# Splitting the attention's row maxima into bf16 parts on GpSimd instead of VectorE

## The chip, the cores and the metric

The kernel runs on one core of a Trainium2 chip. The metric is the device time of one execution in microseconds (us). A core has five engines that each run their own queue of instructions in order and wait for each other by semaphores: TensorE (PE in the profile, its weight loads PEld), VectorE (DVE), ScalarE (ACT), GpSimd (POOL) and SyncE (SP, which here only issues DMAs).

## What is computed

Six residual steps on x of shape 16 x 512 x 128, float32. The change concerns the second, causal attention with 16 heads of width 8 that share 4 key and value heads. Cut to what matters:

```python
x = x + 0.5 * ffn0(layernorm(x))     # per-feature networks of width 16 (called kan)
x = x + attn(layernorm(x))           # below
x = x + 0.5 * ffn0(layernorm(x))
x = x + 0.5 * experts(layernorm(x))  # each of 8 experts takes its 128 best tokens
x = x + recurrence(layernorm(x))
x = x + 0.5 * experts(layernorm(x))

# attn
att = einsum('bhqd,bhkd->bhqk', q, k) * HD ** -0.5   # q and k rotated, HD = 8
att = where(causal, att, lowest)
y = einsum('bhqk,bhkd->bhqd', softmax(att), v) @ Wo
```

The softmax needs each query's largest score subtracted before the exponential.

## The kernel before

**Packed operands.** To keep float32 accuracy with bf16 matmuls, q and k are each split into three bf16 parts, and the nine products are laid along the contraction: 9 x 8 = 72 rows. A packed tile of queries QP (10 of them, one per batch row and key head) and of keys KP (3 of them) has 72 rows of parts, and further down, at rows 96 to 98 (`MXR = 96`, L31), three rows for the row maximum. In QP these three rows hold the three bf16 parts of *minus* the maximum of each query; in KP they hold ones (`keys_cleared`, L503). So the matmul of scores over rows 0 to 98 (`ROWS`, L188) gives score minus maximum at once, and the exponential needs no bias per query.

**Two passes.** For each of the 16 batch rows b, `maxima` (L597) multiplies the 72 rows into PSUM (tile ps_sc, L611), and VectorE reduces each bank to row maxima (L616 with the causal mask, L621 for several heads at once). After each half (two of four key heads, 8 heads) `max_rows` (L625) makes the three parts: ms part 0 is the bf16 of minus the maximum, r the rest, part 1 the bf16 of r, part 2 what then remains. TensorE transposes ms into ps_m (L642), VectorE copies that to mr (L644), and SP sends it through DRAM into rows 96 to 98 of two QP tiles (L649, L651). One batch row later, `weights` (L657) multiplies 99 rows (ps_st, L669), ScalarE takes the exponential into pt (L672), and GpSimd zeroes the upper triangle of the diagonal block (L674). `outputs` (L680) multiplies pt by the values (ps_av, L692).

**The order of work.** The order on TensorE, ScalarE, VectorE and GpSimd is written out by the kernel. A loop of turns, 44 per batch row (one for each of 11 banks of each key head), issues one bank of `weights` of row b and one bank of `maxima` of row b + 1. Then `turn` (L1104) gives one step first to each generator in the list urgent (`max_rows` and `outputs`) and then to each in sides: the stages of other rows, such as `kan` (L329), `attn_in` (L415, rotation and splitting of q and k, with GpSimd sums rope_a, L440, rope_ka, L463, and `parts`, L393), `stage_out`, the layer norms (`norm`, L280) and the top-8 routing. A step asks by `need(...)` (L221) for a share of an engine's budget per turn, and waits for a later turn if what is left is too little:

```python
MOST = {"pe": 1.5, "dve": 1.15, "act": 0.85, "pool": 1.45}   # L218
while paced[0] and any(w > room[e] for e, w in work.items()):
    yield
```

The rope sums ask for pool=1.25, the steps of `parts` for 1.15 to 1.3, a layer norm for dve=0.6 and pool=1.4. A PSUM bank of the two that the side stages share is asked for by `bank` (L243). Half 0 of row b + 1 is finished in the middle of the turns of row b, half 1 at the start of those of row b + 1.

After the 16 rows come the experts and the recurrence, with no attention work left (from about 960 us on).

The functions that are touched, and what calls them:

## Time and profile before

| | |
|---|---|
| median of 3 runs | 1685.1 us (1683.93 to 1688.63) |
| profiled execution | 1679.07 us, span 1677.3 us |
| mean granted TensorE clock | 0.979 of full speed |
| instructions in the profile | 35404 |
| attention's matmuls of scores, ps_sc L611 and ps_st L669 | 259.6 and 258.5 us busy, 1024 each |
| row maxima, L616 on VectorE | 315.0 us busy, 512 |
| masking, L674 on GpSimd | 252.7 us busy, 704 |

The profile lists busy times by engine, groups of equal instructions by line of the kernel (out<-in by tile names, count, busy us, mean ns, and the idle time before them with what ended it), and the chain of work that ended last. A timeline row has start and duration in us, the engine, the line and the tiles; in brackets the idle time before it and what it waited for. "Busy" for TensorE comes from modelled ends: a matmul's row is longer than the distance at which the next can start, so distances between starts are read for its waits.

### The profile page before, as it was taken

Reading aid. Unit: us, or ns where it says so; the run is one execution under the profiler, and the core shown is the slowest. Engines: PE = TensorE matmul, PEld = TensorE weight load, DVE = VectorE, ACT = ScalarE, POOL = GpSimd, SP = SyncE. Lnnn points to the kernel's source line nnn. Section 1 sums busy time; section 2 is a strip of 40 time slices with the busy share of each in tenths; the row PEclk is TensorE's granted clock in tenths of the full one; section 3 lists DMA queues with packets and bytes.
Section 4 is the critical chain, followed back from the end, with each engine's and each line's share of the span. In section 5 each row is a group of like instructions: output and inputs, shape, how many; then the busy total and the mean of one; then the engine's idle time right before and its main releaser. Section 6 shows DMA issues by size and latency. Waiting matters only on the chain.

```text
span 1677.3 us, 35404 instructions
## 1 busy us (share of the span) xinstructions
PE 1573.0 (94%) x12943; PEld 1093.7 (65%) x12943; DVE 1124.6 (67%) x3606; ACT 1002.3 (60%) x2000; POOL 1023.6 (61%) x1486
## 2 busy tenths in 40 slices
PE   5689999999999999999999799999999999999998
PEld 2234444444444544455444399888998889999998
DVE  6578878888888888888986146843469544672222
ACT  3446677787777877777777565444443434444454
POOL 2635557556665556565634757657766668667774
PEclk9779999999999999999999799999999999999999
DMA  4210111111101110111122114223323233333333
GB/s 123 67 63 26 56 50 40 33 42 57 53 30 40 49 57 23 40 52 56 35 81 62 30 40 78 58 52 76 64 59 64 58 61 73 67 64 75 70 77 58
DMA packets 103093, 94.87 MB, mean 57 GB/s; under 512 B 13197, under 2 KB 91478, under 8 KB 102678
## 3 DMA queue, kind: packets, MB, share of 16 engines
q1 hardware_dynamic: 76060, 67.65, 13.1%
q0 software_dynamic: 26048, 24.93, 9.4%
q8 instruction: 102, 1.67, 0.4%
q14 instruction: 73, 0.60, 0.1%
q10 hardware_dynamic: 810, 0.02, 0.0%
HBM read 59.00 MB, written 37.49 MB: 58 GB/s over the span
## 4 chain that ended last, share of the span: by engine, by line
PE 71%; DVE 19%; ACT 5%; issue 3%; POOL 2%; DMA 1%; DVEq 0%; SPq 0%; POOLq 0%; ACTq 0%
PE ps_h L935 12%; PE ps_y L950 11%; PE ps_av L692 7%; PE ps_st L669 6%; PE ps_sc L611 5%; DVE below L616 5%; PE acc L968 4%; PE ps_kg L365 4%; PE ps_s L338 3%; PE ps_t L318 3%; DVE ln_st L287 2%; ACT pt L672 2%; PE ps_ko L386 2%; PE ps_h L1076 2%; PE ps_h L1075 1%
## 5 line engine op out<-in xcount | busy, mean ns | idle before, releaser
L674 POOL TENSOR_SCALAR_AFFINE_SELECT pt<-pt 128x128 f32<-128x128 f32 (+2 forms) x704 | 252.7, 366 | 331.4 <-ACT pt L672 326.6
L672 ACT ACTIVATE pt<-ps_st 128x512 f32<-128x512 f32 (+1 forms) x704 | 378.8, 563 | 99.8 <-PE ps_st L669 94.0
L616 DVE CUSTOM_DVE_ANT_0 below<-ps_sc,causal 128x512 bf16<-128x512 f32 (+1 forms) x512 | 315.0, 615 | 80.1 <-PE ps_sc L611 64.8
L937 ACT ACTIVATE mo<-ps_h 128x512 f32<-128x512 f32 x256 | 152.8, 597 | 290.4 <-PE ps_h L935 288.5
L859 POOL DMA_INDIRECT xg<-xnd,tokI x256 | 252.3, 986 | 80.9 <-issue 45.0
L669 PE MATMUL ps_st<-qp,kp 99*128 99x512 bf16 (+3 forms) x1024 | 258.5, 305 | 21.7 <-ACT pt L672 20.8
L935 PE MATMUL ps_h<-xin,mw 128*128 128x128 f32 x2048 | 278.3, 279 | 0.0
L950 PE MATMUL ps_y<-mw,mo 128*128 128x128 f32 x2048 | 271.1, 275 | 0.4 <-DVE mo L959 0.4
L611 PE MATMUL ps_sc<-kp,qp 72*128 72x512 bf16 (+3 forms) x1024 | 259.6, 305 | 11.6 <-DVE maxs L616 6.6
L935 PEld LDWEIGHTS ps_h<-xin,mw 128*128 128x128 f32 x2048 | 249.7, 192 | 6.1 <-issue 3.2
L950 PEld LDWEIGHTS ps_y<-mw,mo 128*128 128x128 f32 x2048 | 249.1, 192 | 1.5 <-DVE mo L959 1.3
L982 POOL DMA_INDIRECT sum<-ye,tokI x124 | 201.4, 1624 | 63.4 <-ACT ye L953 22.7
L669 PEld LDWEIGHTS <-kp 99*128 99x128 bf16 x1024 | 95.1, 100 | 181.7 <-issue 164.4
L371 ACT ACTIVATE kan_h<-kan_s,rbias,kw 128x512 f32<-128x512 f32 x256 | 205.7, 812 | 3.8 <-PE ps_kg L365 3.8
L692 PE MATMUL ps_av<-pt,va 128*32 128x512 f32 (+3 forms) x2048 | 165.5, 441 | 0.0
L621 DVE TENSOR_REDUCE maxs<-ps_sc 128x2 f32<-128x512 f32 (+1 forms) x192 | 130.1, 685 | 34.9 <-PE ps_sc L611 34.4
L611 PEld LDWEIGHTS <-qp 72*128 72x128 bf16 x1024 | 96.2, 99 | 79.8 <-issue 57.2
L956 DVE TENSOR_TENSOR mo<-mo 128x128 bf16<-128x128 f32 x132 | 38.2, 290 | 129.4 <-ACT mo L941 129.1
L692 PEld LDWEIGHTS ps_av<-pt,va 128*32 128x32 f32 x2048 | 53.7, 109 | 94.9 <-issue 44.1
L968 PE MATMUL acc<-mo 128*128 128x128 bf16 x1584 | 111.3, 219 | 3.1 <-DVE mo L956 3.0
L968 PEld LDWEIGHTS <-mo 128*128 128x128 bf16 x1584 | 98.6, 98 | 19.9 <-issue 18.6
L294 POOL TENSOR_TENSOR ln_rstd<-ln_rstd,mhalf 128x4 f32<-128x4 f32 x96 | 101.1, 1053 | 8.0
(197 smaller groups left out, 2362.2 us busy)
## 6 DMA issues: line engine op xcount, KB each, us to landing
qp<-qs SPq DMA_DIRECT2D x64, 288.0 KB
xnd<-kan_x SPq DMA_DIRECT2D x32, 256.0 KB
sum<-x SPq DMA_DIRECT2D x31, 256.0 KB
qs<-qpart SPq DMA_DIRECT2D x48, 128.0 KB
kp<-ks SPq DMA_DIRECT2D x48, 96.0 KB
x<-in_L_attn_x_dram SPq DMA_DIRECT2D x16, 256.0 KB
mw<-in_L_ffn_w_dram SPq DMA_DIRECT2D x16, 256.0 KB
xg<-xnd,tokI POOLq DMA_INDIRECT x256
```

The costliest lines, as they stand in the source:

```text
L371: nc.scalar.activation(h, sk[half], AF.Relu, bias=rbias[:, half, v : v + 1], scale=kw1[:, half, v : v + 1])
L611: nc.tensor.matmul(v[:, u, 0:n], lhsT=qp[r][0 : 9 * HD, g, bass.ts(c, P)], rhs=kp[0 : 9 * HD, r, 0:n], start=alone, stop=(u == len(gs) - 1 ...
L616: nc.vector.tensor_tensor_reduce(below[:, 0:n], v[:, 0, 0:n], causal[:, S - n : S], 1.0, LOWEST, ALU.add, ALU.max, accum_out=maxs[:, c, h ...
L669: nc.tensor.matmul(v[:, u, 0:n], lhsT=kp[ROWS, r, bass.ts(c, P)], rhs=qp[r][ROWS, g, c * P : S], start=True, stop=True)
L672: nc.scalar.activation(o, v[:, :, 0:n], AF.Exp, scale=HD ** -0.5)
L674: nc.gpsimd.affine_select(out=dg, in_=dg, compare_op=ALU.is_ge, fill=0.0, base=0, pattern=[[0, len(gs)], [1, P]], channel_multiplier=-1)
L692: nc.tensor.matmul(po[32 * g : 32 * g + 32, c * P : S], lhsT=va[:, c, r, :], rhs=pt[:, g, OFF[c] : OFF[c] + n], start=(c == 0), stop=(c == ...
L859: nc.gpsimd.indirect_dma_start(out=xgs[i // E % 2][:, i % E, :], out_offset=None, in_=xnd[b], in_offset=bass.IndirectOffsetOnAxis(ap=tokI[ ...
L935: nc.tensor.matmul(pst[:, f, :], lhsT=mw1[e][:, bass.ts(f, P)], rhs=xins[i // E % 2][:, i % E, :], start=True, stop=True)
L950: nc.tensor.matmul(py, lhsT=hs[u][:, f, :], rhs=mw2[e][:, f, :], start=(f == 0), stop=(f == NF - 1))
L968: nc.tensor.matmul(acc[:, c, :], lhsT=sels[u][:, bass.ts(c, P)], rhs=yes[u][:, w, :], start=(e == 0 and c == 0 and w == 0), stop=(e == las ...
L982: nc.gpsimd.indirect_dma_start(out=sums[k, b], out_offset=bass.IndirectOffsetOnAxis(ap=tokI[g][:, n : n + 1], axis=0), in_=ye[:, b % 2 * ( ...
```

## The change

GpSimd makes the parts instead of VectorE, the parts keep the sign of the maximum, and the keys' three rows hold minus ones instead of ones. The two requests to the turn's budget ask for GpSimd instead of VectorE. Since `max_rows` steps before the side stages in a turn, the order of the side stages' work follows from what is left of each budget.

```diff
@@ -503,7 +503,7 @@
         def keys_cleared(i):
 
             cleared(KP[i])
-            nc.vector.memset(KP[i][MXR : MXR + 3, :, :], 1.0)
+            nc.vector.memset(KP[i][MXR : MXR + 3, :, :], -1.0)
@@ -625,16 +625,15 @@
         def max_rows(b, half, maxs):
 
             H2 = NH // 2
-            yield from need(dve=0.45)
+            yield from need(pool=0.5)
             ms = w2p.tile([P, NT, 3, H2], BF16, name="ms")
             r = w2p.tile([P, NT, H2], F32, name="ms_r")
-            nc.vector.tensor_scalar_mul(ms[:, :, 0, :], maxs, -1.0)
-            nc.vector.scalar_tensor_tensor(r, in0=maxs, scalar=-1.0, in1=ms[:, :, 0, :],
-                                           op0=ALU.mult, op1=ALU.subtract)
-            yield
-            yield from need(dve=0.45)
-            nc.vector.tensor_copy(ms[:, :, 1, :], r)
-            nc.vector.tensor_sub(ms[:, :, 2, :], r, ms[:, :, 1, :])
+            nc.gpsimd.tensor_copy(ms[:, :, 0, :], maxs)
+            nc.gpsimd.tensor_tensor(r, maxs, ms[:, :, 0, :], ALU.subtract)
+            yield
+            yield from need(pool=0.5)
+            nc.gpsimd.tensor_copy(ms[:, :, 1, :], r)
+            nc.gpsimd.tensor_tensor(ms[:, :, 2, :], r, ms[:, :, 1, :], ALU.subtract)
             yield
             yield
             pm = yield from bank([3 * H2, NT, P], BF16, "ps_m", 0.3)
```

The changed file is one line shorter from there on, so L640 and later of the kernel before are one less in it.

## The prediction

> **What bounds the kernel now.** I read the page's busy table and its chain first, then the table of engine times for one steady batch, then the groups by shape, and last the timeline around two sets of row maxima.

> The page:

> ```profile
> PE 1573.0 (94%) x12943; PEld 1093.7 (65%) x12943; DVE 1124.6 (67%) x3606; ACT 1002.3 (60%) x2000; POOL 1023.6 (61%) x1486
> ...
> PE 71%; DVE 19%; ACT 5%; issue 3%; POOL 2%; DMA 1%; DVEq 0%; SPq 0%; POOLq 0%; ACTq 0%
> ```

> TensorE carries the chain, but VectorE has a fifth of it, and GpSimd almost nothing. Engine times over one steady batch (columns: PE, PEld, DVE, ACT, POOL busy us with counts, granted clock, DMA share, GB/s):

> ```profile
> 320.40:374.20 53.80, 51.47 (x399) 26.13 (x399) 45.34 (x143) 42.24 (x77) 33.08 (x64) 1.00 0.13 45
> ```

> TensorE is busy for 96% of 53.8 us at full clock, VectorE for 84%, GpSimd for 61%. So VectorE time as such is not what a batch costs. Only the moments count in which TensorE, which runs its queue in order, waits for VectorE. The groups by shape, with the four VectorE steps that go and the GpSimd rows nearest to what comes:

> ```profile
> L632 DVE SCALAR_TENSOR_TENSOR ms_r<-maxs,ms 128x32 f32<-128x32 f32 x32 | 13.7, 429 | 1.1
> L637 DVE TENSOR_TENSOR ms<-ms_r,ms 128x32 bf16<-128x32 f32 x32 | 13.0, 407 | 1.1
> ...
> L631 DVE TENSOR_SCALAR ms<-maxs 128x32 bf16<-128x32 f32 x32 | 8.0, 251 | 0.0
> L636 DVE CAST ms<-ms_r 128x32 bf16<-128x32 f32 x32 | 7.3, 227 | 0.0
> ...
> L293 POOL TENSOR_SCALAR ln_rstd<-ln_mv 128x4 f32<-128x4 f32 x96 | 21.9, 229 | 127.2 <-DVE ln_mv L291 127.0
> ...
> L399 POOL TENSOR_TENSOR qpart<-rope_a,qpart 128x512 bf16<-128x512 f32 x16 | 18.5, 1157 | 0.6 <-ACT qpart L396 0.6
> ```

> The view of the tile ms gives medians of 176, 193, 176 and 193 ns for L631, L632, L636 and L637. The means of L632 and L637 are more than twice that, so some are held up. The timeline shows where (start us, duration us; half 1 of the maxima, at the start of a batch; I call it set A):

> ```profile
> 320.70 1.28 POOL L440 TENSOR_TENSOR rope_a<-rope_a,rope_b 128x512 f32<-128x512 f32 x1
> ...
> 320.81 1.22 DVE L632 SCALAR_TENSOR_TENSOR ms_r<-maxs,ms 128x32 f32<-128x32 f32 x1
> ...
> 323.46 1.15 POOL L399 TENSOR_TENSOR qpart<-rope_a,qpart 128x512 bf16<-128x512 f32 x1
> ...
> 323.60 1.06 DVE L637 TENSOR_TENSOR ms<-ms_r,ms 128x32 bf16<-128x32 f32 x1
> ...
> 323.83 0.38 PE L611 MATMUL ps_sc<-kp,qp 72*128 72x512 bf16 x1
> ...
> 324.72 0.39 PE L642 MATMUL ps_m<-identb,ms 128*24 128x128 bf16 x4 [0.51 <-DVE ms L637]
> ...
> 325.05 0.34 PE L669 MATMUL ps_st<-qp,kp 99*128 99x384 bf16 x1
> ...
> 325.52 0.32 PE L611 MATMUL ps_sc<-kp,qp 72*128 72x384 bf16 x1
> ```

> Each VectorE step with two SBUF inputs that meets a GpSimd step with two inputs ends just after it: L632 at 322.03, L440 at 321.98; L637 at 324.66, L399 at 324.61. It repeats in 7 sets A, at 266.9, 320.8, 374.7, 428.6, 482.3, 536.1 and 590.0, with 1.22 and 1.06 us each time. TensorE pays: back to back, 512 columns start 0.22 apart, so L642 could start at 324.05 and starts 0.67 later; then L611 starts 0.47 after L669 where 384 columns need 0.16, 0.31 lost, and a turn later (327.21 to 327.58) another 0.21, both for the VectorE maxima that the hold pushed back. Together 1.19 us per set A.

> **The change, part by part.** *Removed from VectorE:* 32 sets of four steps, 8.0 + 13.7 + 7.3 + 13.0 = 42.0 us; undisturbed 32 x 0.738 = 23.6, so 18.4 are holding. On the path: 7 x 1.19 = 8.3 us in the sets A. In the 7 sets B (half 0, mid-batch) TensorE does not wait for ms, so 0. The other 18 sets (7 before 266 us, 11 after 643) lie in batches in which TensorE waits for VectorE elsewhere (maxima, the top-8 steps); bounds 0 and the whole 0.74 each. TensorE has little VectorE-made waiting per batch, so I stay near the low end: 0.15 x 18 = 2.7 us.

> *Added to GpSimd:* per set two casts and two subtractions on 32 elements. No row has these. For a cast the nearest is L293, 229 ns for 4 elements. For a subtraction: from 230 fixed to L399's 1157 at 512 is 1.81 ns an element, so 230 + 58 = 290 (an estimate). Between dependent GpSimd steps the trace shows 0.09 us (L293 ends 315.01, L294 starts 315.10). A pair costs 0.61 us, a set 1.22, all sets 39 us. Bounds: 0.10 a step (the smallest memsets) to 1.05 (L294's power on 4 elements); I take the estimate, since L293 has the same make. [...] The rows say that in a set A VectorE itself takes 0.17 + 1.22 + 0.18 + 1.06 = 2.63, [...]

> *The new wait:* each pair stands behind its turn's L674, which waits for ACT's exponential. Queued behind it are the next L674 and the rope steps; waiting for it is TensorE's L642. A set B of the trace tells the margin:

> ```profile
> 351.02 0.29 POOL L674 TENSOR_SCALAR_AFFINE_SELECT pt<-pt 128x128 f32<-128x128 f32 x1 [1.38 <-ACT pt L672]
> ...
> 351.69 0.38 PE L611 MATMUL ps_sc<-kp,qp 72*128 72x512 bf16 x1
> ...
> 352.00 0.39 PE L642 MATMUL ps_m<-identb,ms 128*24 128x128 bf16 x4
> ```

> The second pair runs from 351.31 to 351.92, plus some 0.05 of signalling; L642 could start at 351.91. So the margin is about zero. In the changed program's order the second half of ps_s (L338, two passes 0.43 apart, 0.86 us) stands ahead of L642 in sets B from batch 4 on, which covers it. Without that cover I take 0.05 (bounds 0 and 0.3) on 25 sets: +1.2 us. The later L674 wait for nobody: GpSimd idles 0.8 to 1.4 us ahead of nearly each.

> *What moves:* GpSimd's budget of 1.45 a turn falls to 0.95 in two turns of a set. In sets A the rope sum (1.25) no longer fits, and goes two turns later, as do its parts and their DMAs to qs and ks on SP; the total of turns stays the same, and the keys are wanted some 20 turns later, so that lateness is covered. pk's bank is held two turns longer: ps_v goes from the turn before ps_av to the one after, L642 one turn later (which removes any wait there), ps_kg, ps_t and ps_ko swap around it, and from the fifth turn all are level again. A turn without a filler (0.43 us of TensorE against ACT's 0.6 and VectorE's 0.77) then comes earlier. Bounds: 0 to 0.5 per batch for a new wait, 0 to -0.58 for the wait of ps_t on L709 at 332.29 (the layer-norm statistics that stand ahead of L709 there now come after it). I take +0.1 in 12 batches, 1.2 us, and -0.2 in 7, 1.4 us. The memset of -1 costs what that of 1 did, and the products are the same.

> Sum: -8.3 - 2.7 + 1.2 + 1.2 - 1.4 = -10.0 us. Against the profiled execution's 1679.1 (span 1677.3 and 1.8 around it) that is 1669.1; the median of the runs stands 6.0 above it, so 1675 us.

> **Rivals.** *Forecast, 0.58:* as summed, 1664 to 1679.

> *The stall only changes its name, 0.26:* when TensorE no longer waits for ms, it meets ACT's exponentials sooner (1.4 us of waits per steady batch end on them already), and the empty turn that the rope shift makes eats the rest. For it: ACT is busy 42 of 53.8 us. Against it: the two turns after L642 wait for VectorE alone. 8 of the 10 us come back, 1683.

> *GpSimd hands over late, 0.16, slower:* in the 18 sets outside the steady stretch nothing stands between the second pair and L642. At 0.8 us a step (L294 takes 1.05, a 512-wide subtraction 1.16) a pair is 1.7, L642 is late by 1.7 + 0.05 - 0.60 = 1.15, 20.7 us in 18 sets, and 1.15 - 0.86 = 0.29 in the 7 sets B, 2.0; less the 11.2 us that the other terms gain, +11.5, 1697. It decides from a step of about 0.55 us on, where late hand-over eats the gain, and is slower by 0.3% from 0.7. Against it: L293's 229.

> **Numbers.** A measurement here tells some 0.3%, 5 us, from no change. Faster 0.58, same 0.26, slower 0.16. The low end, 1664, has 8.3, the wait on L709 whole (4.1), 0.5 in each of the 18 sets (9.0) and no cost; the high end, 1691, is the slower rival at 0.7 us a step (0.94 x 18 + 0.1 x 7 - 11.2 = +6). About 0.08 is left out below and 0.11 above.

> **What will show it.** Right: no VectorE step of 1.2 us in sets A; L642 starts 0.22 after its neighbour; a steady batch takes about 52.6 instead of 53.8 us; GpSimd's four rows average 0.2 to 0.3 us; VectorE busy falls by some 42 us. Wrong: TensorE waits for a GpSimd ms ahead of L642; GpSimd rows over 0.5 us; batch length unchanged with more waiting on ACT's pt; new holds of L308 behind GpSimd's steps; longer batches after 643 us, where the order of the norms changes.

## The result, and the profile after

The changed kernel takes 1709.5 us (median of 4 runs, 1704.9 to 1714.3) against 1684.6 us for the kernel before on the same chip: a ratio of 1.0147, with an interval of 1.0116 to 1.0178. It is 1.5% slower, where 0.6% faster was forecast. The profiled execution took 1707.76 us with a span of 1706.0 (before: 1679.07 and 1677.3). Its mean granted clock is 0.954, against 0.979.

The page of the changed kernel, with the busy times, the row of the granted clock, and the chain:

```profile
PE 1602.2 (94%) x12943; PEld 1117.0 (65%) x12943; DVE 1107.2 (65%) x3478; ACT 1001.4 (59%) x2000; POOL 1047.5 (61%) x1614
...
PEclk9779989988999899999999999999998999999999
...
PE 75%; DVE 15%; ACT 4%; issue 3%; POOL 2%; DMA 1%; SPq 0%; DVEq 0%; POOLq 0%; ACTq 0%
```

128 instructions left VectorE and came to GpSimd, as planned. VectorE's share of the chain fell from 19% to 15%, yet TensorE is busy 29 us longer (1573.0 before) with the same 12943 matmuls, at the lower granted clock. The row of the clock in the kernel before:

```profile
PEclk9779999999999999999999799999999999999999
```

Slices 6, 9, 10, 14 and 31 (of 42.7 us each) hold an 8 where the kernel before has a 9. Slices 9, 10 and 14 lie in the steady batches, slice 31 in the part after the attention. Engine times of one such batch of the changed kernel (columns as in the prediction: busy us with counts of PE, PEld, DVE, ACT and POOL, granted clock, DMA share, GB/s):

```profile
385.60:441.90 56.30, 54.03 (x397) 28.91 (x395) 43.15 (x134) 41.44 (x76) 33.53 (x71) 0.91 0.13 43
```

The batch takes 56.3 us instead of 53.8 although VectorE does 2.2 us less in it, and its granted clock is 0.91 instead of 1.00. Reading the spans between the same masking steps, the 28.7 us of difference between the two profiled executions divide as follows.

| stretch (before; after) | before | after | difference | clock before, after |
|---|---|---|---|---|
| to the first steady batch (266.6; 273.4) | 266.6 | 273.4 | +6.8 | 0.90, 0.88 |
| six steady batches (to 589.7; 611.2) | 323.1 | 337.8 | +14.7 | 1.00, 0.93 |
| the rest of the attention (to 956.3; 980.2) | 366.6 | 369.0 | +2.4 | 0.98, 0.97 |
| experts and recurrence | 721.0 | 725.8 | +4.8 | 1.00, 0.99 |

The last stretch holds no row maxima. A second profile of the unchanged kernel (b_again, further down) takes 727.0 us there, more than the changed kernel. Both have 10.2 us at half clock there (from 1279.4 us, and from 1298.8 us in the changed kernel), which the first profile of before lacks. So the 4.8 us also come without the change. Of the other 23.9 us, 14.7 are in the steady batches.

Is it GpSimd's steps? The view of the tile ms in the changed kernel (minimum, median and maximum in ns, first and last start):

```profile
L631 POOL CAST ms<-maxs x32: 199/212/1035, 96.2 to 934.2; 128x32 bf16<-128x32 f32 x32
L632 POOL TENSOR_TENSOR ms_r<-maxs,ms x32: 245/247/1025, 96.5 to 934.5; 128x32 f32<-128x32 f32 x32
L635 POOL CAST ms<-ms_r x32: 207/212/665, 96.8 to 935.2; 128x32 bf16<-128x32 f32 x32
L636 POOL TENSOR_TENSOR ms<-ms_r,ms x32: 244/246/248, 97.1 to 935.5; 128x32 bf16<-128x32 f32 x32
```

No: in the median they take 0.21 and 0.25 us, a little less than the 0.23 and 0.29 forecast, and in the steady batches the distances between TensorE's starts show no wait for ms any more. What is new there is a wait for a layer norm. In the kernel before, the last step of a gating layer norm (L304: x times a factor plus a shift per token, on 128 x 128 float32 of one tensor) met one GpSimd step. Its timeline (start and duration in us):

```profile
340.55 1.27 POOL L375 TENSOR_TENSOR x<-x,kcst 128x512 f32<-128x512 f32 x1
...
341.12 1.04 DVE L304 TENSOR_SCALAR kan_x<-x,ln_mv,ln_rstd 128x128 f32<-128x128 f32 x2
```

The row joins two steps, of 0.78 and 0.33 us: the first is held until L375 ends at 341.82, and TensorE needs neither yet. The same norm in the changed kernel:

```profile
345.79 1.63 DVE L304 TENSOR_SCALAR kan_x<-x,ln_mv,ln_rstd 128x128 f32<-128x128 f32 x2
345.92 1.15 POOL L402 TENSOR_TENSOR rope_ka<-rope_ka,kpart 32x512 f32<-32x512 f32 x1
...
347.30 1.15 POOL L405 TENSOR_TENSOR kpart<-rope_ka,kpart 32x512 bf16<-32x512 f32 x1
...
347.95 2.32 DVE L304 TENSOR_SCALAR kan_x<-x,ln_mv,ln_rstd 128x128 f32<-128x128 f32 x2
...
348.41 0.28 POOL L673 TENSOR_SCALAR_AFFINE_SELECT pt<-pt 128x128 f32<-128x128 f32 x1
...
348.67 1.25 POOL L375 TENSOR_TENSOR x<-x,kcst 128x512 f32<-128x512 f32 x1
...
350.07 0.73 PE L318 MATMUL ps_t<-ident,kan_x 128*128 128x128 f32 x2 [1.44 <-DVE kan_x L304]
...
350.59 0.53 PE L668 MATMUL ps_st<-qp,kp 99*128 99x384 bf16 x1
```

The first of the four L304 steps takes 1.37 us and ends just after L402. The third starts at 347.95 and takes 2.06 us, where an undisturbed one takes 0.34: it is held over L405, L673 and L375, which run back to back, and ends at 350.01, just after L375 (349.92). TensorE has two of the four transposes (L318) behind it and waits. By the distances between starts, the third transpose comes 1.7 us after the instruction before it in each of eight batches from 294 to 690 us. From then on TensorE is slow: the next 384 columns (L668) take 0.53 us, where the same shape takes 0.33 a few rows earlier. Windows of 3.4 us around the wait (columns as above):

```profile
346.50:349.90 3.40, 1.65 (x22) 0.74 (x13) 3.40 (x5) 2.30 (x5) 3.40 (x6) 0.99 0.20 79
349.90:360.10 10.20, 10.03 (x48) 6.46 (x49) 6.18 (x25) 5.02 (x9) 3.53 (x10) 0.50 0.25 89
360.10:363.50 3.40, 3.40 (x19) 1.24 (x18) 2.46 (x6) 3.22 (x7) 1.50 (x7) 1.00 0.20 76
```

After a window in which TensorE was busy for less than half, the granted clock is 0.50 for 10.2 us. In each of the eight batches such a stretch, 3.4 to 10.2 us long, begins between 0.2 us before and 1.7 us after the end of that wait (at 295.2, 349.9, 407.9, 465.9, 520.5, 575.1, 633.2 and 691.2 us). The stretches at half clock that begin between 120 and 990 us last 95.6 us in all, against 23.9 in the kernel before.

### The profile page after: what moved, and what is told of

It is laid out like the page before. It is cut to its first block, busy times and chain, and to the rows that moved or that the text cites. A ratio compares the mean times of both kernels' runs of the same rounds, so it can differ in the third digit from the quotient of the medians.

```text
span 1706.0 us, 35447 instructions
## 1 busy us (share of the span) xinstructions
PE 1602.2 (94%) x12943; PEld 1117.0 (65%) x12943; DVE 1107.2 (65%) x3478; ACT 1001.4 (59%) x2000; POOL 1047.5 (61%) x1614
## 4 chain that ended last, share of the span: by engine, by line
PE 75%; DVE 15%; ACT 4%; issue 3%; POOL 2%; DMA 1%; SPq 0%; DVEq 0%; POOLq 0%; ACTq 0%
PE ps_h L934 12%; PE ps_y L949 11%; PE ps_st L668 7%; PE ps_av L691 7%; PE ps_sc L611 7%; PE acc L967 4%; PE ps_kg L365 4%; DVE below L616 3%; PE ps_s L338 3%; PE ps_t L318 3%; ACT pt L671 2%; PE ps_g L743 2%; PE ps_h L1075 2%; PE ps_h L1074 2%; PE ps_ko L386 2%
## 5 line engine op out<-in xcount | busy, mean ns | idle before, releaser
L673 POOL TENSOR_SCALAR_AFFINE_SELECT pt<-pt 128x128 f32<-128x128 f32 (+2 forms) x704 | 246.8, 357 | 313.1 <-ACT pt L671 306.8
L611 PE MATMUL ps_sc<-kp,qp 72*128 72x512 bf16 (+3 forms) x1024 | 267.6, 314 | 13.9 <-DVE maxs L616 10.9
L668 PE MATMUL ps_st<-qp,kp 99*128 99x512 bf16 (+3 forms) x1024 | 265.1, 312 | 16.2 <-ACT pt L671 15.6
L668 PEld LDWEIGHTS <-kp 99*128 99x128 bf16 x1024 | 97.2, 103 | 189.9 <-issue 175.2
L611 PEld LDWEIGHTS <-qp 72*128 72x128 bf16 x1024 | 99.2, 102 | 72.4 <-issue 48.3
L955 DVE TENSOR_TENSOR mo<-mo 128x128 bf16<-128x128 f32 x132 | 38.2, 290 | 129.0 <-ACT mo L940 127.2
L691 PEld LDWEIGHTS ps_av<-pt,va 128*32 128x32 f32 x2048 | 53.9, 110 | 94.8 <-issue 65.4
L967 PEld LDWEIGHTS <-mo 128*128 128x128 bf16 x1584 | 99.1, 98 | 19.7 <-issue 18.4
L293 POOL TENSOR_SCALAR ln_rstd<-ln_mv 128x4 f32<-128x4 f32 x96 | 21.9, 228 | 144.6 <-DVE ln_mv L291 144.5
```

What stands on the lines that cost most here:

```text
L611: nc.tensor.matmul(v[:, u, 0:n], lhsT=qp[r][0 : 9 * HD, g, bass.ts(c, P)], rhs=kp[0 : 9 * HD, r, 0:n], start=alone, stop=(u == len(gs) - 1 ...
L668: nc.tensor.matmul(v[:, u, 0:n], lhsT=kp[ROWS, r, bass.ts(c, P)], rhs=qp[r][ROWS, g, c * P : S], start=True, stop=True)
L673: nc.gpsimd.affine_select(out=dg, in_=dg, compare_op=ALU.is_ge, fill=0.0, base=0, pattern=[[0, len(gs)], [1, P]], channel_multiplier=-1)
L691: nc.tensor.matmul(po[32 * g : 32 * g + 32, c * P : S], lhsT=va[:, c, r, :], rhs=pt[:, g, OFF[c] : OFF[c] + n], start=(c == 0), stop=(c == ...
L967: nc.tensor.matmul(acc[:, c, :], lhsT=sels[u][:, bass.ts(c, P)], rhs=yes[u][:, w, :], start=(e == 0 and c == 0 and w == 0), stop=(e == las ...
```

## The experiments

**Theory O (order).** The parts on GpSimd are fine. Their request for pool=0.5 leaves 0.95 of 1.45 of GpSimd's budget, so in those turns no rope sum (1.25) or part (1.15 to 1.3) fits. The side stages' steps then change places, and the last key parts (L402, L405) and L375 (x plus the constant term of a stage) come to lie beside L304. The hold makes TensorE wait, and the wait halves the clock. **The rivals.** GpSimd: the four steps themselves cost the time, by a late hand-over or by holding other VectorE steps. Waits alone: the hold costs what TensorE waits, and the lower clock is chance.

The experiments ran on two chips. The unchanged kernel took 1709.7 us on the one (e1 to e4) and 1682.3 on the other (the rest), so only ratios to its time on the same chip are compared. The changed kernel itself was not run again beside them; its ratio stays 1.0147.

**e1_old_order: the steps on GpSimd, the order of before.**

```diff
-            yield from need(pool=0.5)
+            yield from need(dve=0.45)
```

This is the changed kernel with both requests as they were; all else then stands in the old order.

> GpSimd makes the parts as in the change, but the two requests are need(dve=0.45) as before, so the side stages keep exactly the order of the kernel before. Theory O (the request to GpSimd's budget moves the rope parts next to the layer norm's L304, whose hold leaves TensorE idle 1.6 us a batch and its clock halved after it): no L304 over 0.8 us in a batch, granted clock about 0.979, time 8 us below before, 1674 to 1680. Rival H (the small GpSimd steps hand over late or hold the queue): slow as the change, 1700 to 1712.

Measured: 1705.8 against 1709.7 us, ratio 0.9985 (0.9967 to 1.0004). The loss is gone, as Theory O says, but the 8 us of gain that were expected are not there: the time cannot be told from that of before. Engine times of its batch:

```profile
329.30:382.10 52.80, 51.18 (x402) 26.30 (x398) 41.79 (x135) 42.22 (x77) 34.16 (x73) 1.00 0.14 45
```

A steady batch takes 52.8 us, 1.05 less than before, at full clock. So in the old order the steps bring in the steady stretch what was forecast, and the loss does not come from them. Over the whole kernel little is left of six times 1.05: the stretch up to the first steady batch takes 8.3 us longer than in the first profile of before (274.9 against 266.6). There GpSimd does hand over late. TensorE's matmuls wait 3.2 us for L636 in the first rows (where the kernel before waits 0.8 for its VectorE counterpart). The timeline of the longest of these waits:

```profile
165.99 1.25 POOL L463 TENSOR_TENSOR rope_ka<-rope_ka,rope_kb 32x512 f32<-32x512 f32 x1
...
167.20 0.87 POOL L673 TENSOR_SCALAR_AFFINE_SELECT pt<-pt 128x512 f32<-128x512 f32 x2
...
168.04 0.20 POOL L631 CAST ms<-maxs 128x32 bf16<-128x32 f32 x1
...
169.06 0.24 POOL L636 TENSOR_TENSOR ms<-ms_r,ms 128x32 bf16<-128x32 f32 x1
...
169.36 0.39 PE L641 MATMUL ps_m<-identb,ms 128*24 128x128 bf16 x4 [2.48 <-POOL ms L636]
```

The four steps take little; GpSimd has no idle time ahead of them, and a rope sum and two masking steps stand in its queue first.

**e2_new_order: the steps on VectorE, the order of the changed kernel.** The converse, in the kernel before:

```diff
-            yield from need(dve=0.45)
+            yield from need(pool=0.5)
```

> VectorE makes the parts as before, but requests need(pool=0.5) twice, so the side stages have exactly the order of the changed kernel. Theory O: L304 of 1.4 and 2.1 us as in the change, granted clock about 0.95, time 1705 to 1720. Rival H: as before, 1680 to 1690.

Measured: 1730.9 against 1709.7 us, ratio 1.0142 (1.0100 to 1.0183). A batch takes 56.5 us, with the same hold. The view of L304 in this kernel:

```profile
L304 DVE TENSOR_SCALAR kan_x<-x,ln_mv,ln_rstd x192: 317/341/2058, 229.1 to 1472.3; 128x128 f32<-128x128 f32 x192
...
  PE ps_t L318: 11.5, 8
```

The longest L304 takes 2058 ns, and TensorE's matmuls wait for it 8 times, 11.5 us in all. Not one instruction of the maxima has moved to GpSimd here, and within the intervals the loss is that of the whole change. The rival GpSimd falls for the steady stretch.

**e3_wider_budget: the change, with room for the rope sum beside the new request.**

```diff
-        MOST = {"pe": 1.5, "dve": 1.15, "act": 0.85, "pool": 1.45}
+        MOST = {"pe": 1.5, "dve": 1.15, "act": 0.85, "pool": 1.95}
```

> The change, with GpSimd's budget of a turn raised from 1.45 to 1.95, so that a pair of parts fits beside a rope sum (1.25) or a norm (1.4). Theory O: the rope parts are no longer put off; if L304 stays under 0.8 us, clock 0.975 and 1672 to 1690; if the wider budget puts other GpSimd sums beside L304, it is slow again. Rival H: 1700 to 1715.

Measured: 1701.7 against 1709.7 us, ratio 0.9952 (0.9935 to 0.9969), with a batch of 52.8 us. With 1.95 - 0.5 = 1.45 left, the sum fits in the turn where it was. This is the change as it was meant, and it is 0.5% faster than before. A second way of taking the shift away has the same batch as e1_old_order.

**e4_filler: the change, with TensorE kept at work in the wait.** Ahead of the four transposes of a gating layer norm, seven extra matmuls whose result is overwritten (98 in all, so in 14 of the 16 rows):

```diff
+            for _ in range(7 if busy and paced[0] else 0):
+                nc.tensor.matmul(ps.rearrange("p c q -> p (c q)"), lhsT=identb, rhs=causal, start=True, stop=True)
```

> The change, with seven bf16 matmuls of 512 columns, whose result is overwritten, ahead of the transposes that wait for L304 in the gating norm of each of the 16 rows: 1.5 us more of TensorE work a row, in the place where TensorE stands idle 1.6 us. If the idle time is what halves the clock: the low-clock stretches between 150 and 700 us go, clock 0.97 or more, time 15 to 25 us below the change, 1685 to 1695, though TensorE has more to do. If the wait alone costs (rival S): as the change or up to 7 us slower, 1708 to 1718.

Measured: 1713.4 against 1709.7 us, ratio 1.0029 (1.0010 to 1.0047). Its batch:

```profile
329.30:382.90 53.60, 52.26 (x407) 27.21 (x407) 44.07 (x135) 41.98 (x77) 34.08 (x73) 1.00 0.14 45
```

More work makes it faster than the change: a batch takes 53.6 us instead of 56.3, at full clock. The hold is still there (the longest L304 takes 2064 ns), as is the order. So the wait, filled with work, costs under 1 us a batch beyond e1_old_order, and the lower clock that it brings is most of the loss. The rival of waits alone falls.

**b_again: the kernel before once more, with a profile.**

> The kernel before once more, for a profile beside the other runs of this chip: low-clock time between 120 and 990 us near 24 us, a steady batch of 53.8 us, L304 under 0.8 us there, whatever the theory.

Measured: 1689.65 us in its one run. It has a stretch of 10.2 us at half clock near 225 us, which the first profile of before lacks, and its mark at the first steady batch is 271.0 us instead of 266.6. Its half clock between 120 and 990 us is 37.5 us (counted as above), not near 24 as expected. So about half of the 8.3 us that e1_old_order loses there also comes in the unchanged kernel. With single executions on each side, this split is argued, not shown.

**e5_late_kcst: the change, with L375 alone three turns later.**

```diff
-                if t == 1:
+                if t == 4:
```

The request for it stays where it was, so no other instruction moves.

> The change, with GpSimd's sum x + kcst (L375, 1.25 us) issued three steps later in its stage, its request to the budget left where it was, so nothing else moves. It is one of the GpSimd steps behind which the third L304 of a batch is held. Theory O: that L304 falls from 2.06 to 0.7 us or less, TensorE's wait for it from 1.6 to 0.3 us or less, most low-clock stretches between 280 and 700 us go, ratio to before 0.998 to 1.006 instead of 1.0147. If another part of the new order is the cause: ratio 1.011 to 1.016.

Measured: 1681.9 against 1682.3 us, ratio 0.9976 (0.9960 to 0.9993), with a batch of 52.6 us. The view of L304:

```profile
L304 DVE TENSOR_SCALAR kan_x<-x,ln_mv,ln_rstd x192: 321/341/1384, 238.3 to 1441.8; 128x128 f32<-128x128 f32 x192
...
  PE ps_t L318: 1.3, 8
```

The longest L304 now takes 1384 ns, as the one beside L402 did, and the matmuls of L318 wait 1.3 us for it in all, not 11.5. The third L304 of the batch (two in one row here, of 0.58 and 0.57 us) ends just after L405:

```profile
349.30 1.15 POOL L405 TENSOR_TENSOR kpart<-rope_ka,kpart 32x512 bf16<-32x512 f32 x1
...
349.96 1.07 DVE L304 TENSOR_SCALAR kan_x<-x,ln_mv,ln_rstd 128x128 f32<-128x128 f32 x2
```

The kpart steps still lie beside L304, and they alone do not bring the clock down: in the six batches it is low for 3.4 us once. Moving one GpSimd step of 1.25 us by three turns takes the whole 1.5% back.

**e6_wide_late and e7_old_late: VectorE for the first four rows, GpSimd from then on.** e6_wide_late has the budget of e3_wider_budget, e7_old_late the requests of e1_old_order. The core of the edit:

```diff
+            eng, work = (nc.vector, {"dve": 0.45}) if b < 4 else (nc.gpsimd, {"pool": 0.5})
+            yield from need(**work)
...
-            nc.gpsimd.tensor_copy(ms[:, :, 0, :], maxs)
+            eng.tensor_copy(ms[:, :, 0, :], maxs)
```

> The wider budget (1.95) with GpSimd from row 4 on and VectorE (the same positive parts, need(dve=0.45)) for rows 0 to 3, where GpSimd handed over up to 2.6 us late in the run with the old order. If that late hand-over, and the low clock after it, is what took back the gain of the steady batches: marks before 266 us as before, 6 to 8 us below the run with the wider budget, ratio to before 0.989 to 0.994. If not: 0.994 to 0.997 as with the wider budget alone.

> The old order (need(dve=0.45)), VectorE for rows 0 to 3, GpSimd from row 4 on. By the same reasoning ratio to before 0.993 to 0.997, against 0.9985 with GpSimd for all rows; if the early hand-over is not the cause, 0.997 to 1.000.

Measured: e6_wide_late 1672.7 against 1682.3 us, ratio 0.9936 (0.9913 to 0.9959), the lowest of all; e7_old_late 1680.5, ratio 0.9977 (0.9963 to 0.9992). The first ratio lies in the range that was expected, the second misses it (0.993 to 0.997). The steady batches take 52.8 us in both, but for the first of the six (53.8 and 53.9). Against e3_wider_budget (0.9952) and e1_old_order (0.9985) both are lower, but the intervals overlap, so the times do not settle what avoiding the late hand-over is worth. The traces say more. The first steady batch begins at 266.6 to 271.0 us in the five that make the first rows' parts on VectorE (before, b_again, e2, e6, e7), and at 273.4 to 278.8 in the five that make them on GpSimd: 6.5 us apart in the mean, in either order. In the first rows, then, the rival GpSimd stands. How much of that is the wait for L636 and how much the clock after it was not separated.

## Why the prediction was wrong

*The step that failed is "What moves".* It allowed the order shift +1.2 us less 1.4, with bounds of 0 to 0.5 us per batch for a new wait. Measured, the changed kernel's six steady batches take 337.8 us where the same steps in the old order (e1_old_order) take 316.8: 3.5 us per batch, seven times the upper bound. The step did see that the rope sum and the parts go turns later. It then asked only who waits for their results (keys, a bank, L709), not beside what they come to lie, and it held that "from the fifth turn all are level again". They are not. In the kernel before (a batch that begins at 320.4) the gating norm's statistics (L291) come with the last key part, 17.2 us into the batch:

```profile
337.58 0.37 DVE L291 BATCH_NORM_AGGREGATE ln_mv<-ln_st 128x2 f32<-128x6 f32 x4
337.58 1.15 POOL L405 TENSOR_TENSOR kpart<-rope_ka,kpart 32x512 bf16<-32x512 f32 x1
```

In the changed kernel (from 329.3) they come at 13.2 us, some three turns of 1.2 us earlier, and ahead of the key parts:

```profile
342.48 0.37 DVE L291 BATCH_NORM_AGGREGATE ln_mv<-ln_st 128x2 f32<-128x6 f32 x4
```

The norm has overtaken the parts that were put off: its first L304 moves from 20.7 to 16.5 us, while L405 moves from 17.2 to 18.0. That is how they meet. Two things more were missing.

- *Who can be held.* The prediction spoke of VectorE steps "with two SBUF inputs". L304 has one tensor in SBUF, and the trace of before already showed it held: 0.78 us instead of 0.34 beside L375 in a steady batch, up to 0.82 elsewhere. A hold that ends with one GpSimd step, as L632's and L637's in the sets A did, leaves at most 1.25 + 0.34 = 1.6 us, an estimate from the longest such row in the timeline (1.25 us for L375) and the 0.34 of L304 itself. The trace has 2.06, across three steps in a row, and the measurement decides.
- *The clock.* The sum took full clock for granted, though the trace of before has a clock of 0.90 up to its first steady batch. The stall of 1.6 us (1.7 less the 0.11 between the starts of two undisturbed transposes) became a loss of 3.5 us per batch: at a clock of 0.93 over the six batches, 0.07 x 56.3 = 3.9 us of TensorE's time are missing, and some of it comes back because other waits of its matmuls shrink (from the kernel before to the changed kernel those for ACT's exponentials from 0.9 to 0.3 us per batch, those for L709 from 0.4 to none).

*Point by point.*

- Stall on ms in the sets A, 1.19 us each: right in mechanism and nearly in size, 1.05 us per batch (e1_old_order).
- GpSimd's price of 0.229 and 0.290 us a step: right, 0.212 and 0.247. The sets B saw no late hand-over in the steady stretch.
- The 18 other sets, -2.7 and +0.9 us: wrong in sign for the first rows, where TensorE's matmuls wait 3.2 us for L636 instead of 0.8 for L637. The slower rival had this mechanism, but with a step of 0.7 us as its cause. The cause is what is queued on GpSimd ahead of the steps.
- VectorE's busy time, -42 us forecast: it fell by 17.4 us (1124.6 to 1107.2), since holds count as busy: L304 alone rose from 61.0 to 80.6 us. In e1_old_order it fell by 35.0.
- The wait on L709: gone in the changed order. Of its 0.58 us per batch 0.2 had been entered; neither matters beside 3.5.
- The total: e3_wider_budget, which leaves the order alone, is 0.5% faster, near the 0.6% forecast. The terms are not those of the sum: the steady batches give 6.3 us (323.1 to 316.8), and the first rows, from which a gain was forecast, cost. So the nearness is in part luck.
- The rivals: none of the three cases described what happened. The range ended at 1691, since its upper end was a mishap of the new steps and not of the old ones that they displace.
- The signs to look for named "new holds of L308 behind GpSimd's steps": the right kind of sign, at the wrong line and with no price.

## What to carry to other kernels

When a step asks for a share of an engine's budget, price what it displaces: list the instructions that move, those that come earlier too, and for each the steps of the other engines beside which it will lie, not only who reads its result. Read the minimum, median and maximum of a group: here a maximum of twice the median (L304 in the kernel before, 822 ns against 336) was a hold, and several neighbours in a row held the same step for longer than any one of them (2.06 us, where the longest, L375, took 1.25). The TensorE stall had two prices here. Over the six steady batches (316.8 us in e1_old_order, 321.0 in e4_filler, 337.8 in the changed kernel) the filled wait cost 0.7 us a batch and the clock afterwards 2.8. A cheap edit that moves one instruction (L375) or fills the wait tells which of them it is.

## What the runs showed of the hardware

**The clock was halved after half-busy windows.** In the traces of the kernels before and after, every stretch at one granted clock lasts 3.41 us or a whole multiple of it (6.83, 10.24, up to 713.4 us), but for the last, which the end of the trace cuts short. I laid a grid of such windows through these changes, took TensorE's busy time in each window at full clock from 100 to 900 us, in the ten traces of this case, and counted how often half clock followed in the next.

| busy in the window of 3.41 us | windows | followed by half clock |
|---|---|---|
| under 1.95 us | 31 | 31 |
| 1.95 to 2.3 us | 34 | 17 |
| 2.3 to 2.9 us | 215 | 19 |
| over 2.9 us | 1925 | 0 |

**A hold can outlast the GpSimd step that began it.** The third L304 waited through L405, L673 and L375, 2.06 us where 0.34 is normal; so it did in e2_new_order (2058 ns) and e4_filler (2064 ns). With L375 moved away (e5_late_kcst) it took 0.58 us and ended just after L405. By the recorded times L375 began 0.22 us after L405 had ended, so why the step did not end between the two in the changed kernel stays open.

**Small GpSimd casts and subtractions cost little more than on VectorE.** A cast of 32 elements took 212 ns and a subtraction of 32 took 247, in the median; VectorE's for the same were 176 and 193 ns. An addition on 4 elements (L293) took 229 ns in the mean. Not every small step is cheap: the power on 4 elements (L294) took 1053.
